# Reordered stages, later projection products and a row-by-row last product in a two-layer graph kernel on one Trainium2 core

## The chip, the cores and the metric

The kernel runs on one core of a Trainium2 chip. A core has five engines with instruction streams of their own: TensorE (PE, matrix products into PSUM), VectorE (DVE), ScalarE (ACT), GpSimd (POOL) and SyncE (SP, here only a queue that starts transfers). Each engine works through its own stream in order and waits on semaphores where it needs what another engine makes. The metric is the device time of one execution in microseconds (us); lower is better. The timed value is the median of several executions.

## The reference

Two graph layers act on `x` (4096 x 512) with one 4096 x 4096 adjacency matrix, everything in float32:

```python
def _L0_gnn_ref(cur, incidence_m):
    mask = incidence_m > 0
    head = mask.astype(incidence_m.dtype)
    head = head / jnp.maximum(jnp.sqrt(jnp.sum(head * head, axis=-1, keepdims=True)), EPS)
    inc = incidence_m + head
    return (inc @ cur) / jnp.sum(inc, axis=-1, keepdims=True)

def _L1_gnn_ref(X, A, W):
    A2 = A + jnp.eye(A.shape[0], dtype=A.dtype)
    dscale = jnp.diagonal(A2) ** (-0.5)
    temp = A2 @ X @ W.T
    A_norm = dscale[:, None] * A2 * dscale[None, :]
    return jax.nn.relu(A_norm @ temp)

x = _layernorm(x + _L0_gnn_ref(x, adj), axis=-1)
x = _layernorm(x + _L1_gnn_ref(x, adj, L1_gnn_W), axis=-1)
```

So there are three large products: `inc @ cur`, `A2 @ X`, and `A_norm @ temp`. The product by `W.T` (512 x 512) lies between the second and the third.

## The kernel before

**Tiling.** The first product (line 526 in the profile) uses one level of a Strassen-Winograd scheme: 7 products of blocks in place of 8. The second and third product (line 295) use two levels. The outer level has 7 products `p`, the inner level 7 products `m`. The work of these two phases is one list of steps `(k, s, p, kk)`: `k` is 2 for `A2 @ X` and 3 for `A_norm @ temp`, `s` is one of two strips, `p` runs through `ORDER[k]` (for `k = 3`: 2, 3, 5, 1, 6, 7, 4), and `kk` runs from 0 to 7 over the contraction. A step issues 7 matmuls, one for each inner product `m`, of 128 x 128 stationary values and 512 moving columns, into PSUM banks 0 to 6 (`q0` to `q6`). A float32 matmul stands in the profile as two records. After `kk = 7` the function `outer` combines the seven banks into the result blocks `c11, c12, c21, c22` on DVE.

**Bank 7.** The eighth PSUM bank (`spare`, line 96) serves everything else that PE does: the products by `W.T` (line 829) and the transposes of finished blocks (`turn_back`, line 903). There is one of it, so the next user waits until ACT has read the one before it.

**The order of a step** is written out by hand (`manual_schedule`); no scheduler moves anything. In the loop of line 1101 step `n` issues: loads; `prepare(n + 2)`, three DVE additions (lines 170, 172, 173) that make the sums for the matmuls two steps ahead; `sum_b` for the stationary side; operations put off by `outer` (`deferred`, line 1115, each over 128 x 2048 values); the 7 matmuls, between which `between[m]` puts other PE work ahead of matmul `m`; what is left of `items`; and then, lines 1144 to 1146, one further stage of the output rows under way.

**Rows under way.** When a block of the third product is finished, its rows leave through `layer1` (line 922): transposes on PE into bank 7, `rectify` on ACT (line 907, reads bank 7), then two stages, each run in a later step: `measured` (DVE: add the residual, line 758, and take statistics, lines 936 and 937) and `rest` (ACT: square root, line 940; DVE: reciprocal `rs` and offset `nb`, lines 162 and 164; ACT: `o*rs+nb`, line 165; a store). In the last product of all (`p = 4` of the last strip, `end` is true) up to two items are taken per step: one ahead of matmul 3, one after the matmuls. Its last rows go through `layer1_first` (line 945: transposes of the finished half, ACT line 957, and the stages `divided`, ACT line 962, and `rest`, DVE lines 758 and 970).

**Products by `W.T`.** `project` (line 813) is a generator. Two blocks are under way per outer product, one begun at `kk = 2` (`first`) and one at `kk = 4`. Each yields small tables `{m: product}` that say ahead of which matmul of the step a product goes. The seven products of a block are spread over three steps; ACT copies each from bank 7 (line 831); POOL makes four sums of blocks (line 836 and on) between the first table and the second; DVE combines the seven copies at the end (lines 858 to 867).

**The end.** For the last `TAIL = 4` steps of the last product no matmuls are issued in the loop; `finish` (line 973) does them product by product: `multiply(m)` runs the four remaining matmuls of one inner product, and DVE and ACT combine each while the next runs. The last one, `q4` (index 6), is needed for one quarter of the block. After it DVE subtracts it (line 1069), PE transposes four blocks of 128 x 128 (`turn`, line 993), and DVE and ACT take the layer norm (lines 1001 to 1023) and store through SP (line 1025).

Of the kernel before, what the change touches and what calls it, by code (L numbers as in the profile page):

```python
# [10 lines left out]
AF = mybir.ActivationFunctionType  # L11
ALU = mybir.AluOpType

P = 128
# [6 lines left out]
B11, B21, B22, T1, T2, T3, T4 = range(7)  # L21
# [5 lines left out]
def tile_adj_resnorm_d2(  # L27
# [37 lines left out]
    nc = tc.nc  # L65
# [12 lines left out]
    NQ = NB // 4  # L78
# [13 lines left out]
    def bank(m):  # L92

        return psum.tile([P, D], F32, tag=f"q{m}", name=f"q{m}")
# [4 lines left out]
    def row_tile(tag, bufs, shape=(P, D)):  # L99
        return rows.tile(list(shape), F32, tag=tag, name=tag, bufs=bufs)  # L100


    ident = const.tile([P, P], F32, name="ident")
# [76 lines left out]
    TAIL = 4  # L180
# [14 lines left out]
    steps = [(k, s, p, kk) for k in (2, 3) for s in range(NS) for p in ORDER[k] for kk in range(NQ)]  # L195
# [3 lines left out]
    resident, loaded, ready, raw_b, sums_b = {}, {}, {}, {}, {}  # L199
    made = {"a": 0, "s": 0, "load": 0, "load_b": 0}  # L200
    going, leaving = [], []
    queue, pairs, later, deferred, raises, stores = [], [], [], [], [], []
# [87 lines left out]
    def multiply2(n, acc, between):  # L290
        kk = steps[n][3]
        for m, (right, left) in enumerate(factors(n)):
            if m in between:
                between[m]()
            nc.tensor.matmul(acc[m], left, right, start=(kk == 0), stop=(kk == NQ - 1))  # L295

    def load_up_to(n):
        while made["load"] <= min(n, len(steps) - 1):
# [243 lines left out]
    def take(h, acc):  # L542

        y = row_tile("z", 2)
        nc.scalar.copy(y[:, 0:H], acc[0][:, 0:H])
        nc.scalar.copy(y[:, H:D], acc[1][:, 0:H])
        nc.scalar.copy(degrees[0][:, h:h + 1], acc[0][:, H:H + 1])
        return y
# [67 lines left out]
    ps = spare()  # L616
# [3 lines left out]
    for c in range(NC):  # L620
        m = count_half(0, c, ps)
# [135 lines left out]
    def add(o, y):  # L757
        nc.vector.tensor_add(o, o, y)  # L758
# [54 lines left out]
    def project(h, s, n, first):  # L813

        cols = slice(n * P, (n + 1) * P)
        a11, a12, a21, a22 = (C_of[2][h][f][:, 2 * r:2 * r + 2, cols] for r in range(2) for f in range(2))
        if first:
            pools["places"] = [t[:, i * H:(i + 1) * H] for t in (row_tile(t, 1) for t in ("p1", "p5", "u2", "u3")) for i in range(2)]  # L820

        places = [pools["places"][i] for i in (range(7) if first else (7, 1, 0, 6, 3, 2, 4))]
        q = []

        def product(left, right):
            def now():
                ps = spare()[:, 0:H]
                for e in range(2):
                    nc.tensor.matmul(ps, left[:, e, :], wt[:, right, e, :], start=(e == 0), stop=(e == 1))
                q.append(places[len(q)])  # L830
                nc.scalar.copy(q[-1], ps)
            return now

        def sums():
            s1, s2, s3, s4 = (y[:, 2 * i:2 * i + 2, :] for y in (row_tile("y", 2, (P, 4, P)) for _ in range(2)) for i in range(2))
            nc.gpsimd.tensor_add(s1, a21, a22)  # L836
            nc.gpsimd.tensor_add(s2, a11, s1)
            nc.gpsimd.tensor_add(s3, a11, a21)
            nc.gpsimd.tensor_add(s4, a12, s2)
            return s1, s2, s3, s4  # L840

        if first:
            yield {1: product(a11, B11), 3: product(a12, B21), 5: product(a22, T4)}
            s1, s2, s3, s4 = sums()
            yield
            yield {1: product(s2, T2), 3: product(s3, T3), 5: product(s1, T1)}
            yield
            yield {1: product(s4, B22)}
        else:
            yield {4: product(a11, B11)}  # L850
            s1, s2, s3, s4 = sums()
            yield
            yield {1: product(a12, B21), 3: product(a22, T4), 5: product(s2, T2)}
            yield
            yield {1: product(s3, T3), 3: product(s1, T1), 5: product(s4, B22)}
        q1, q2, q4, q6, q7, q5, q3 = q
        z = [row_tile("z", 2) for _ in range(2)]
        nc.vector.tensor_add(z[0][:, 0:H], q2, q1)
        nc.vector.tensor_add(q6, q6, q1)
        nc.vector.tensor_add(q7, q7, q6)  # L860
        nc.vector.tensor_add(q6, q6, q5)
        nc.vector.tensor_add(z[0][:, H:D], q3, q6)
        nc.vector.tensor_sub(z[1][:, 0:H], q4, q7)
        nc.vector.scalar_tensor_tensor(z[1][:, H:D], q7, -1.0, q5, op0=ALU.mult, op1=ALU.subtract)
        t = row_tile("t", 1, (P, 4, H))
        for r in range(2):
            nc.vector.tensor_sub(t[:, 2 * r, :], z[r][:, 0:H], z[r][:, H:D])
        leaving.extend(lambda r=r: leave_operands(h, r * NQ + s * SB + n, z[r], t[:, 2 * r, :]) for r in range(2))
        yield
# [103 lines left out]
    def finish(h, items, acc):  # L973

        c21 = C_of[3][h][0]
        q1, q2, q6, q5, q7, q3, q4 = range(7)
        p1, p5, u2 = (row_tile(t, 1) for t in ("p1", "p5", "u2"))
        e0, e1 = row_tile("y", 2), row_tile("y", 2)  # L980
        tail = [(steps[n][3], factors(n)) for n in range(len(steps) - TAIL, len(steps))]
        first = [items[r * SB][0] + h * NP for r in range(2)]
# [3 lines left out]
        def multiply(m, of=slice(0, TAIL)):  # L986
            for kk, f in tail[of]:
                right, left = f[m]
                nc.tensor.matmul(acc[m], left, right, start=False, stop=(kk == NQ - 1))  # L989

        def turn(r, n, i, o):

            nc.tensor.transpose(o, c21[:, 2 * r + i, n * P:(n + 1) * P], ident)  # L993
# [5 lines left out]
        def take(r, n, f, ps):  # L999
            y, o = rows_of(r, n)  # L1000
            nc.vector.scalar_tensor_tensor(o[:, :, f], ps, 0.0, y[:, :, f], op0=ALU.max, op1=ALU.add)

        def measure(r, n, i, w):
            nc.vector.bn_stats(late["st", r][:, n, i, :], rows_of(r, n // 2 * 2)[1][:, n % 2, i * w:(i + 1) * w])  # L1004

        def deviation(r, lo, hi):
            for n in range(lo, hi):
                nc.vector.bn_aggr(mean[r][:, n, :], late["st", r][:, n])
            nc.vector.tensor_add(dev[r][:, lo:hi], mean[r][:, lo:hi, 1], late["eps"][:, first[r] + lo:first[r] + hi])
            nc.scalar.activation(dev[r][:, lo:hi], dev[r][:, lo:hi], AF.Sqrt)  # L1010
# [6 lines left out]
        def leave(r, n, by_act):  # L1017
            o = rows_of(r, n // 2 * 2)[1][:, n % 2, :]
            rs = dev[r][:, n:n + 1]
            if by_act:  # L1020
                nc.scalar.activation(o, o, AF.Identity, scale=rs, bias=off[r][:, n:n + 1])  # L1021
            else:
                nc.vector.tensor_scalar(o, o, mean[r][:, n, 0:1], rs, op0=ALU.subtract, op1=ALU.mult)
            b = first[r] + n
            nc.sync.dma_start(out=out[b * P:(b + 1) * P, :], in_=o)
# [8 lines left out]
        nc.vector.tensor_sub(c21[:, 2, :], u2, c21[:, 2, :])  # L1034
        multiply(q5)
        nc.scalar.copy(p5, acc[q5])
        add(u2, p5)
        less(e1, u2, c21[:, 1, :])
        nc.vector.tensor_sub(c21[:, 3, :], u2, c21[:, 3, :])
        multiply(q3)  # L1040
        nc.vector.tensor_sub(c21[:, 1, :], e1, acc[q3])
        multiply(q7, slice(0, 1))

        for n in (0, 2):
# [3 lines left out]
                    turn(0, n + i, e, ps[:, i, e * P:(e + 1) * P])  # L1048
            take(0, n, slice(0, H), ps)
        multiply(q7, slice(1, TAIL))  # L1050
        for n in range(4):
            measure(0, n, 0, H)
        deviation(0, 0, 4)
# [1 line left out]
        invert(0, 0, 4)  # L1055
        for n in range(4):
            leave(0, n, True)
        nc.vector.tensor_add(c21[:, 2, :], c21[:, 2, :], acc[q7])

        multiply(q4, slice(0, TAIL - 1))  # L1060
        ps = bank(1).rearrange("p (n d) -> p n d", n=4)
        for n in range(4):
            turn(1, n, 1, ps[:, n, :])
        for n in (0, 2):
            take(1, n, slice(P, H), ps[:, n:n + 2, :])
        multiply(q4, slice(TAIL - 1, TAIL))
        for n in (0, 2):
            cols = slice(n * P, (n + 2) * P)
            nc.vector.tensor_sub(c21[:, 2, cols], c21[:, 2, cols], acc[q4][:, cols])  # L1069
        for n in (0, 2):  # L1070
            ps = bank((2, 3)[n // 2]).rearrange("p (n d) -> p n d", n=4)
            for i in range(2):
                turn(1, n + i, 0, ps[:, i, :])
                measure(1, n + i, 1, P)
            take(1, n, slice(0, P), ps[:, 0:2, :])
        for n in range(2):
            measure(1, n, 0, P)
        deviation(1, 0, 2)
        for n in range(2, 4):
            measure(1, n, 0, P)  # L1080
        invert(1, 0, 2)
        leave(1, 0, True)
        deviation(1, 2, 4)
        leave(1, 1, False)
        invert(1, 2, 4)
# [15 lines left out]
    for n, (k, s, p, kk) in enumerate(steps):  # L1101
# [10 lines left out]
        items = [queue.pop(0) for _ in range(min(len(queue), 2 if end else 1))] if 1 <= kk <= 6 else []  # L1112
        held = later[:]
        later.clear()
        while deferred:
            deferred.pop(0)()
            if not pairs:
                break
# [21 lines left out]
            load_b_up_to(n // 2 + 3)  # L1140
        for item in items:
            take_up(item)

        for stages in held if kk < NQ - 1 else ():
            stages.pop(0)()
        later[:0] = [stages for stages in held if stages]
        for pair in going[::-1]:
            next(pair)
        if kk in (4, 6):
# [72 lines left out]
```

## Time and profile before

| | |
|---|---|
| median of 3 runs | 2273.27 us (2271.16 to 2273.32) |
| the profiled execution | 2272.91 us, of which the span of its instructions is 2271.1 us |
| PE busy | 2251.0 us, 7382 matmul records |
| DVE / ACT / POOL busy | 1846.6 / 538.0 / 301.7 us |
| matmuls of the second and third product (line 295), mean of one record | 592 ns (128x512) |
| products by `W.T` (line 829), mean of one record | 380 ns (128x256) |
| transposes (lines 903, 993), mean of one record | 273, 281 ns (128x128) |
| DVE over 128x2048 (line 762, `less`) | 2.28 us |
| DVE `prepare` (lines 170, 172, 173), mean of each | 1236, 713, 701 ns |

[...] Matmuls overlap, so the distance from one start to the next is shorter: records of 512 columns start 0.43 us apart. "Idle before" is the time in which an engine waited in front of an instruction, with the instruction that released it.

### The profile page before, as it was taken

The numbers are of one execution on the slowest core, as the hardware profiler recorded it, in microseconds if no ns is written. First come the engines' busy times: TensorE is split into PE (matmuls) and PEld (weight loads), VectorE is DVE, ScalarE is ACT, GpSimd is POOL, SyncE is SP. The second block draws the span as 40 slices with busy tenths as digits, with TensorE's granted clock in tenths as the row PEclk, the third lists the DMA queues.
The fourth block names the chain that finished last, engine by engine and source line by source line (L and its number), as shares of the span: only waits on it lengthen the run. The fifth ranks groups of instructions, "written<-read, shape, count | busy, mean of one in ns | idle before, by whom it ended". The sixth has DMA issues, their size and how long they took to land. (4 is left out here: it accounts for less than half of the span.)

```text
span 2271.1 us, 22217 instructions
## 1 busy us (share of the span) xinstructions
PE 2251.0 (99%) x7382; PEld 1382.6 (61%) x7382; DVE 1846.6 (81%) x2620; ACT 538.0 (24%) x1336; POOL 301.7 (13%) x408
## 2 busy tenths in 40 slices
PE   8999999999999999999999999999999999999997
PEld 7888888888888844444555444555544444444443
DVE  6989999989989787888876887987767788766677
ACT  4346546555553000000111100111110011200013
POOL 0111122221121110002112200212210011100001
PEclk9999999999999999999999999999999999999999
DMA  9778888888876575675677767577776687765684
GB/s 311 259 273 289 264 265 285 283 279 285 268 248 218 199 278 207 220 294 186 250 274 217 236 255 258 186 285 269 216 239 226 235 288 278 254 242 221 224 295 153
DMA packets 177043, 568.27 MB, mean 250 GB/s; under 512 B 18064, under 2 KB 54944, under 8 KB 138528
## 3 DMA queue, kind: packets, MB, share of 16 engines
q1 hardware_dynamic: 128832, 459.32, 57.0%
q0 software_dynamic: 32480, 92.85, 13.2%
q10 hardware_dynamic: 15616, 14.69, 1.9%
q8 instruction: 58, 0.95, 0.2%
q14 instruction: 57, 0.47, 0.1%
HBM read 443.04 MB, written 123.74 MB: 250 GB/s over the span
## 5 line engine op out<-in xcount | busy, mean ns | idle before, releaser
L295 PE MATMUL q<-s,ts 128*128 128x512 f32 x1320 | 609.5, 592 | 0.2 <-DVE u L749 0.2
L526 PE MATMUL q<-b,s 128*128 128x256 f32 (+1 forms) x1920 | 453.4, 378 | 0.0
L295 PEld LDWEIGHTS q<-s,ts 128*128 128x128 f32 x1320 | 250.4, 190 | 297.8 <-issue 271.0
L170 DVE TENSOR_TENSOR s<-a 128x1024 f32<-128x1024 f32 x234 | 289.2, 1236 | 165.4 <-PE q L295 142.2
L526 PEld LDWEIGHTS q<-b,s 128*128 128x128 f32 x1920 | 362.7, 189 | 52.0
L526 PE MATMUL q<-b,a 128*128 128x256 f32 (+1 forms) x1440 | 350.5, 379 | 0.0
L295 PE MATMUL q<-a,tr 128*128 128x512 f32 x688 | 327.5, 592 | 0.0
L526 PEld LDWEIGHTS q<-b,a 128*128 128x128 f32 x1440 | 272.7, 189 | 38.3
L295 PE MATMUL q<-s,tr 128*128 128x512 f32 x440 | 224.7, 592 | 0.0
L295 PEld LDWEIGHTS q<-a,tr 128*128 128x128 f32 x688 | 128.8, 190 | 142.1 <-issue 134.9
L350 ACT ACTIVATE nat<-nat,tiny 128x512 f32<-128x512 f32 x240 | 173.4, 723 | 27.3 <-DMA nat<-adj 21.0
L295 PE MATMUL q<-a,ts 128*128 128x512 f32 x344 | 175.9, 593 | 0.0
L172 DVE TENSOR_TENSOR s<-a,s 128x512 f32<-128x512 f32 x234 | 166.8, 713 | 8.0
L173 DVE TENSOR_TENSOR s<-a,s 128x512 f32<-128x512 f32 x234 | 163.9, 701 | 8.0
L747 ACT COPY p<-q 128x512 f32<-128x512 f32 x27 | 15.8, 584 | 649.2 <-PE q L295 649.2
L501 DVE TENSOR_TENSOR a<-a,mask 128x1024 f32<-128x1024 f32 (+1 forms) x127 | 154.5, 1217 | 6.4
L499 DVE SCALAR_TENSOR_TENSOR mask<-a,sc 128x1024 f32<-128x1024 f32 (+2 forms) x129 | 154.2, 1197 | 2.2
L295 PEld LDWEIGHTS q<-s,tr 128*128 128x128 f32 x440 | 83.6, 190 | 91.6 <-issue 81.6
L411 ACT ACTIVATE nat<-nat 128x512 f32<-128x512 f32 x192 | 118.8, 619 | 14.0 <-DMA nat<-adj 13.9
L295 PEld LDWEIGHTS q<-a,ts 128*128 128x128 f32 x344 | 65.2, 190 | 83.0 <-issue 77.5
L836 POOL TENSOR_TENSOR y<-c,c 128x256 f32<-128x256 f32 x16 | 21.5, 1342 | 640.7 <-DVE c L762 391.3
L170 DVE TENSOR_TENSOR s<-r 128x1024 f32<-128x1024 f32 x48 | 59.8, 1245 | 40.5 <-PE q L295 31.8
(218 smaller groups left out, 2121.1 us busy)
## 6 DMA issues: line engine op xcount, KB each, us to landing
a<-adj_r SPq DMA_DIRECT2D x112, 1024.0 KB, 7.1
a<-oa SPq DMA_DIRECT2D x80, 1024.0 KB, 5.4
nat<-adj SPq DMA_DIRECT2D x240, 256.0 KB, 5.9
a<-adj_q SPq DMA_DIRECT2D x60, 1024.0 KB, 6.3
tr<-ob SPq DMA_DIRECT2D x112, 512.0 KB, 4.0
oa<-r SPq DMA_DIRECT2D x32, 1024.0 KB, 9.8
oa<-sr POOLq DMA_DIRECT2D x60, 512.0 KB, 6.8
y<-x POOLq DMA_DIRECT2D x64, 256.0 KB, 5.3
```

The costliest lines, as they stand in the source:

```text
L170: nc.vector.tensor_add(s[:, S3:S1 + 1, :], a[:, A11:A22 + 1, :], a[:, A21, :].unsqueeze(1).to_broadcast([P, 2, w]))
L172: nc.vector.tensor_add(s[:, S2, :], a[:, A11, :], s[:, S1, :])
L173: nc.vector.tensor_add(s[:, S4, :], a[:, A12, :], s[:, S2, :])
L295: nc.tensor.matmul(acc[m], left, right, start=(kk == 0), stop=(kk == NQ - 1))
L350: nc.scalar.activation(y, a, AF.Sign, bias=tiny, scale=2.0 ** 64, accum_out=accum)
L411: nc.scalar.activation(nat, nat, AF.Copy, accum_out=totals[j][:, h, t:t + 1])
L499: nc.vector.scalar_tensor_tensor(m, v, 0.0, s.unsqueeze(1).to_broadcast(list(v.shape)), op0=ALU.is_gt, op1=ALU.mult)
L501: nc.vector.tensor_add(z, z, y)
L526: nc.tensor.matmul(acc[m][:, 0:w], left, b[:, right, 0:w], start=(kk == 0), stop=(kk == NP - 1))
L747: nc.scalar.copy(p1, q1)
L836: nc.gpsimd.tensor_add(s1, a21, a22)
```

## The change

Four edits in the function's body:

1. In the last product (`end`) the stages of rows under way (`go_on`) are issued at the beginning of the step, after `prepare` and `sum_b` and ahead of `deferred`, of the matmuls and of new items. In every other product they stay after the items.
2. `project` issues its products later: the block begun at `kk = 2` has its seven products as 2, 3 and 2 per step in place of 3, 3 and 1; the block begun at `kk = 4` has its first one ahead of matmul 5 in place of 4.
3. The accumulation of `q4` in bank 6 ends four steps early; DVE subtracts that part ahead of `q7` (`c21[:, 2] - acc[q4]`). ACT negates the stationary side of the last four steps in place.
4. In `finish` the last four steps of `q4` are made by `complete_rows(n)` for four row blocks of 128: four matmuls of 128 moving columns with the operands exchanged, so that the result comes out transposed, then two matmuls by the identity that add `c21[:, 2]` and a copy `p7` of `q7`. They replace four matmuls of 512 columns, four transposes, and three DVE operations. The DVE operations behind them stand in a new order.

```diff
--- before.py
+++ after.py
@@ -292,7 +292,9 @@
         for m, (right, left) in enumerate(factors(n)):
             if m in between:
                 between[m]()
-            nc.tensor.matmul(acc[m], left, right, start=(kk == 0), stop=(kk == NQ - 1))
+
+            last = NQ - 1 - (TAIL if n >= len(steps) - NQ and m == 6 else 0)
+            nc.tensor.matmul(acc[m], left, right, start=(kk == 0), stop=(kk == last))
 
     def load_up_to(n):
         while made["load"] <= min(n, len(steps) - 1):
@@ -840,14 +842,14 @@
             return s1, s2, s3, s4
 
         if first:
-            yield {1: product(a11, B11), 3: product(a12, B21), 5: product(a22, T4)}
+            yield {3: product(a11, B11), 5: product(a12, B21)}
             s1, s2, s3, s4 = sums()
             yield
-            yield {1: product(s2, T2), 3: product(s3, T3), 5: product(s1, T1)}
+            yield {1: product(a22, T4), 3: product(s2, T2), 5: product(s3, T3)}
             yield
-            yield {1: product(s4, B22)}
+            yield {1: product(s1, T1), 3: product(s4, B22)}
         else:
-            yield {4: product(a11, B11)}
+            yield {5: product(a11, B11)}
             s1, s2, s3, s4 = sums()
             yield
             yield {1: product(a12, B21), 3: product(a22, T4), 5: product(s2, T2)}
@@ -974,9 +976,10 @@
 
 
 
+
         c21 = C_of[3][h][0]
         q1, q2, q6, q5, q7, q3, q4 = range(7)
-        p1, p5, u2 = (row_tile(t, 1) for t in ("p1", "p5", "u2"))
+        p1, p5, u2, p7 = (row_tile(t, 1) for t in ("p1", "p5", "u2", "u3"))
         e0, e1 = row_tile("y", 2), row_tile("y", 2)
         tail = [(steps[n][3], factors(n)) for n in range(len(steps) - TAIL, len(steps))]
         first = [items[r * SB][0] + h * NP for r in range(2)]
@@ -1034,11 +1037,15 @@
         nc.vector.tensor_sub(c21[:, 2, :], u2, c21[:, 2, :])
         multiply(q5)
         nc.scalar.copy(p5, acc[q5])
+
+        for left in (sums_b[n // 2][:, :, 3, :] for n in range(len(steps) - TAIL, len(steps), 2)):
+            nc.scalar.activation(left, left, AF.Copy, scale=-1.0)
         add(u2, p5)
         less(e1, u2, c21[:, 1, :])
         nc.vector.tensor_sub(c21[:, 3, :], u2, c21[:, 3, :])
         multiply(q3)
         nc.vector.tensor_sub(c21[:, 1, :], e1, acc[q3])
+        nc.vector.tensor_sub(c21[:, 2, :], c21[:, 2, :], acc[q4])
         multiply(q7, slice(0, 1))
 
         for n in (0, 2):
@@ -1048,6 +1055,7 @@
                     turn(0, n + i, e, ps[:, i, e * P:(e + 1) * P])
             take(0, n, slice(0, H), ps)
         multiply(q7, slice(1, TAIL))
+        nc.scalar.copy(p7, acc[q7])
         for n in range(4):
             measure(0, n, 0, H)
         deviation(0, 0, 4)
@@ -1055,31 +1063,39 @@
         invert(0, 0, 4)
         for n in range(4):
             leave(0, n, True)
-        nc.vector.tensor_add(c21[:, 2, :], c21[:, 2, :], acc[q7])
-
-        multiply(q4, slice(0, TAIL - 1))
+
+        def complete_rows(n, ps):
+
+            cols = slice(n * P, (n + 1) * P)
+            for i, (kk, f) in enumerate(tail):
+                right, left = f[q4]
+                nc.tensor.matmul(ps, right[:, cols], left, start=(i == 0), stop=False)
+            nc.tensor.matmul(ps, c21[:, 2, cols], ident, start=False, stop=False)
+            nc.tensor.matmul(ps, p7[:, cols], ident, start=False, stop=True)
+
+
+        ends = [bank(b).rearrange("p (n d) -> p n d", n=4) for b in (2, 3)]
+        complete_rows(0, ends[0][:, 0, :])
         ps = bank(1).rearrange("p (n d) -> p n d", n=4)
         for n in range(4):
             turn(1, n, 1, ps[:, n, :])
         for n in (0, 2):
             take(1, n, slice(P, H), ps[:, n:n + 2, :])
-        multiply(q4, slice(TAIL - 1, TAIL))
-        for n in (0, 2):
-            cols = slice(n * P, (n + 2) * P)
-            nc.vector.tensor_sub(c21[:, 2, cols], c21[:, 2, cols], acc[q4][:, cols])
-        for n in (0, 2):
-            ps = bank((2, 3)[n // 2]).rearrange("p (n d) -> p n d", n=4)
+        complete_rows(1, ends[0][:, 1, :])
+        take(1, 0, slice(0, P), ends[0][:, 0:2, :])
+        for n in range(2):
             for i in range(2):
-                turn(1, n + i, 0, ps[:, i, :])
-                measure(1, n + i, 1, P)
-            take(1, n, slice(0, P), ps[:, 0:2, :])
-        for n in range(2):
-            measure(1, n, 0, P)
+                measure(1, n, i, P)
+        for n in (2, 3):
+            complete_rows(n, ends[1][:, n - 2, :])
         deviation(1, 0, 2)
-        for n in range(2, 4):
-            measure(1, n, 0, P)
+        for n in (2, 3):
+            measure(1, n, 1, P)
+        take(1, 2, slice(0, P), ends[1][:, 0:2, :])
         invert(1, 0, 2)
         leave(1, 0, True)
+        for n in (2, 3):
+            measure(1, n, 0, P)
         deviation(1, 2, 4)
         leave(1, 1, False)
         invert(1, 2, 4)
@@ -1112,6 +1128,14 @@
         items = [queue.pop(0) for _ in range(min(len(queue), 2 if end else 1))] if 1 <= kk <= 6 else []
         held = later[:]
         later.clear()
+
+        def go_on():
+
+            for stages in held if kk < NQ - 1 else ():
+                stages.pop(0)()
+            later[:0] = [stages for stages in held if stages]
+        if end:
+            go_on()
         while deferred:
             deferred.pop(0)()
             if not pairs:
@@ -1140,10 +1164,8 @@
             load_b_up_to(n // 2 + 3)
         for item in items:
             take_up(item)
-
-        for stages in held if kk < NQ - 1 else ():
-            stages.pop(0)()
-        later[:0] = [stages for stages in held if stages]
+        if not end:
+            go_on()
         for pair in going[::-1]:
             next(pair)
         if kk in (4, 6):
```

## Prediction

> **What bounds the kernel now.** I read the first page, then the waits of PE, then the timeline in three places where the change acts.
>
> ```profile
> PE 2251.0 (99%) x7382; PEld 1382.6 (61%) x7382; DVE 1846.6 (81%) x2620; ACT 538.0 (24%) x1336; POOL 301.7 (13%) x408
> ...
> PE q L370 <- ACT sr L350: 6.2, 1, 6.2
> PE q L829 <- DVE c L787: 1.1, 2, 0.8
> PE q L903 <- ACT o L907: 1.0, 1, 1.0
> ...
> PE q L993 <- DVE c L1069: 0.5, 1, 0.5
> PE q L989 <- DVE c L172: 0.5, 1, 0.5
> ```
>
> PE is busy for 99% of the span. Its idle time is the start (6.2 us), the layer norm after its last matmul, and the small waits above. So the change can gain only these waits and some of the end, and every microsecond by which it holds PE up is lost. The columns of the waits are total, times and longest. The wait of 1.0 us stands in the second step (`kk = 1`) of the last product:
>
> ```profile
> 2215.38 2.28 DVE L762 SCALAR_TENSOR_TENSOR c<-c,c 128x2048 f32<-128x2048 f32 x1
> 2217.59 0.16 DVE L162 RECIPROCAL rs<-sd 128x1 f32<-128x1 f32 x1
> 2217.78 0.16 DVE L164 SCALAR_TENSOR_TENSOR nb<-mv,rs 128x1 f32<-128x1 f32 x1
> 2217.97 0.82 ACT L165 ACTIVATE o<-o,nb,rs 128x512 f32<-128x512 f32 x1 [14.02 <-DVE nb L164]
> 2218.70 0.67 ACT L907 ACTIVATE o<-q,dscale 128x512 f32<-128x512 f32 x1
> ...
> 2219.41 1.21 DVE L170 TENSOR_TENSOR s<-a 128x1024 f32<-128x1024 f32 x1
> 2219.41 0.66 PE L903 MATMUL q<-ident,c 128*128 128x128 f32 x4 [0.96 <-ACT o L907]
> ...
> 2221.99 0.16 DVE L162 RECIPROCAL rs<-sd 128x1 f32<-128x1 f32 x1
> 2222.18 0.16 DVE L164 SCALAR_TENSOR_TENSOR nb<-mv,rs 128x1 f32<-128x1 f32 x1
> ...
> 2222.37 0.82 ACT L165 ACTIVATE o<-o,nb,rs 128x512 f32<-128x512 f32 x1 [1.35 <-DVE nb L164]
> ```
>
> Four rows are under way here: A and B from the product before, C and D taken in this step. ACT stands at A's line 165 until DVE has made A's `nb`, which comes after the long `less` (L762). C's `rectify` (L907 at 2218.70) is next in ACT's stream, and D's transposes need bank 7, so PE waits. B's `nb` is made at 2222.18, after the `prepare` of 2219.41, and B's line 165 follows at 2222.37.
>
> ```profile
> 2264.00:2265.00 1.00, 0.00 (x0) 0.00 (x0) 0.97 (x5) 0.86 (x2) 0.00 (x0) 0.98 0.00 0
> 2265.00:2266.00 1.00, 0.00 (x0) 0.00 (x0) 0.84 (x4) 0.57 (x2) 0.00 (x0) 0.50 0.19 74
> ```
>
> These are windows; the third number from the end is PE's clock. PE's last matmul begins before 2262; the clock falls to half at 2265, some 3.2 us later.
>
> [...] The trace shows records of 190 ns, but two such loads behind a transpose take 0.30 us together (PEld at 2233.57), so the second begins 0.11 us after the first[...].
>
> **Edit 2, products by W.T.** The two waits of 1.1 us (0.32 and 0.77) stand ahead of the product at matmul 1 of `kk = 2`, which needs DVE's L787. At matmul 3 it comes two matmuls (1.7 us) later; both waits go: -1.1 us. Number and kind of products stay. Behind a later product wait ACT's copy and then DVE's combination: the seventh copy of the first block comes 1.7 us later. At the first place DVE reaches the combination at 1076.40, while the copy ended at 1071.4, so it would still be in time. POOL's sums are used two matmuls later as well. DVE prepares a step or more ahead and waits for PE here (174.0 us in all at L170), which covers the rest. If that cover is gone, DVE is held by up to 1.7 us, not PE. Cost taken: 0 (0 to +1).
>
> **Edit 1, rows under way.** New order on DVE in `kk = 0`: `prepare`; A's `rs`, `nb`; B's `measured`; `less`. In `kk = 1`: `prepare`, then B's `rs`, `nb`. New order on ACT: A's square root and line 165; B's square root and line 165; only then C's and D's `rectify`. Before, C and D stood ahead of B. The total of DVE up to B's `nb` is unchanged (the same instructions in another order), so B's `nb` stays at 2222.18 and B's line 165 at 2222.37. C's `rectify` follows 0.73 later (2217.97 to 2218.70 before), at 2223.10, and D's transposes 0.71 after that (2218.70 to 2219.41), at 2223.81 in place of 2219.41. So the wait isn't removed but grows by **4.4 us**, to 5.4 us of idle PE. Everything on PE moves with it.
>
> In `kk = 3` the like happens on a small scale. ACT now has C's and D's line 165 and four activations of `divided` (0.61 each) ahead of the first L957. I follow it: `prepare` waits for the sums that PE used in `kk = 2` (free at about 2230.1); it ends at 2232.8; C's line 165 begins at 2233.2; D's square root, `nb` and line 165 at 2234.6; `divided` from 2235.3 to 2237.75; L957 0.6. The next transposes, due at 2233.24 + 4.4 = 2237.64, begin at 2238.4: **+0.75 us** (0 to 1.5). In return DVE is now ahead of PE in `finish`. Before, PE needed 2256.30 - 2233.68 = 22.62 us from its first matmul there to the end of `q7`; its work in it is 48 records at 0.429 and 8 transposes at 0.107, 21.45. The waits of 1.18 us (L172, L1041) go: **-1.2 us**.
>
> **Edits 3 and 4, the end.** Removed after `q7`: 8 records of 512 columns (3.43 us), and, behind the last of them, DVE L1069 (0.75) and four transposes. Added: 4 row blocks of 8 + 4 records of 128 columns. No such float32 record is in the trace. Below: the stream of 128 columns is a quarter of 0.429, 0.107[...], so 12 records take 1.285 us. Above: load and stream without overlap at the load's record, 0.190, so 2.28 us. I take 0.107, because the transposes, which also load 128 columns each, run at 0.107 (four in 0.44). Four blocks and four transposes: 4 x 1.285 + 0.43 = 5.57 us after `q7`, where the matmuls ended at 2260.17, 3.87 after. But less follows. After the last row block: 0.21 to the `take`, then by the durations of before (take 0.33, reciprocal and offset 0.26, two statistics 0.39, two aggregates 0.39, sum 0.16, L1023 0.54, reciprocal and offset 0.40) 2.4 us to the last ACT activation, 0.82 long. That is 5.57 + 0.21 + 2.4 + 0.82 = 9.0 us after `q7`; before it was 2266.30 - 2256.30 = 10.0. **-1.0 us**, and up to +3.0 with the slower records (48 x 0.083 = 4.0). The copy of `q7` on ACT (0.6 us) is covered by eight records (0.86 us); negations and subtraction lie beside `q3` and `q7`. The way from there to the end (4.8 us, stores) I leave.
>
> **Sum** for the profiled execution: -1.1 + 4.4 + 0.75 - 1.2 - 1.0 = +1.85 us, that is 2274.8 from 2272.91. The median is 0.36 above that execution: 2273.27 + 1.85 = 2275.1.
>
> **The clock.** [...] No gap of that length in mid-run is in the trace before. [...]2275.1 + 1.7 = **2276.8 us**.
>
> **Rivals.**
> - The gap without the clock: 2275.1 us. [...] Against: three executions or more are timed, and their median lies between.
> - The other side, slower: records of 128 columns run at the load's 0.190 us. Place: the four row blocks; price +4.0 us, thus 2279.1 without the clock's fall and 2280.8 with it. It decides from 0.056 us more per record (2.7 us over 48) upward, a distance of 0.163 us. For it: records of 190 ns. Against: two such loads start 0.11 us apart.
> - The gap doesn't come, since B's line 165 doesn't stand ahead of C: then 1.1 (W.T), 1.0 (L903), 1.0 (end) and up to 1.2 (`finish`) are gained, some 2269.5 us. For it: DVE makes A's `nb` 2.2 us earlier. Against: B's `nb` still stands behind `less` and `prepare`.
>
> **How the numbers follow.** Gap with the clock's fall 0.47; gap without it 0.33; slow records 0.12; no gap 0.08. A median of this kernel tells about 0.2%, 4.5 us, from no change: below 2268.7 is faster, above 2277.8 slower. Slower: the slow records, and a quarter of the first case[...]: 0.24. Faster: 0.03. Same: 0.73. The range from 2273.0 to 2279.6 leaves out the case without a gap and most of the slow records with a cold clock.
>
> **What would show it.** In the profile after: PE's wait on ACT's rectify at D's transposes of about 5.4 us (near 0 if I am wrong), with B's line 165 directly ahead of C's rectify on ACT; the waits on L787 gone; a clock of 0.5 behind the gap, or not; row blocks of 1.3 us (2.3 in the slow case); waits on L172 and L1041 in `finish` gone. The prediction is wrong if B's `nb` comes before 2219, or if the row blocks take over 2 us.

## The result, and the profile after

The changed kernel takes 2276.85 us (median of 15 runs, 2275.39 to 2278.75), the kernel before 2272.50 us (median of 15 runs, 2271.16 to 2273.94). The ratio is 1.0019, 95% interval 1.0012 to 1.0026: 4.35 us slower, at the edge of what was called no change. The profiled execution of the changed kernel took 2277.67 us, its span is 2275.9 us, 4.8 more than before. Lines of the source below the change stand 2 or more higher (`rectify` is now L909, `less` L764, L1041 is L1047).

First the busy times on the page after:

```profile
PE 2253.7 (99%) x7418; PEld 1387.0 (61%) x7418; DVE 1847.4 (81%) x2618; ACT 538.0 (24%) x1339; POOL 293.9 (13%) x408
```

PE is busy 2.7 us longer than before. It has 36 records more, those of the row blocks at the end, and part of the time is the clock, below. PE's waits after (columns: total, times, longest):

```profile
PE q L372 <- ACT sr L352: 6.3, 2, 6.2
PE q L905 <- ACT o L909: 5.3, 1, 5.3
PE q L831 <- ACT p L833: 1.9, 2, 1.1
PE q L905 <- ACT o L959: 0.5, 1, 0.5
```

The waits on DVE L787, L172 and L1041 are gone. In their place stand one wait of 5.3 us and one of 0.5, which were forecast, and two of 1.9 together, which were not. The timeline of the second step of the last product, ACT and PE after:

```profile
2216.53 0.81 ACT L165 ACTIVATE o<-o,nb,rs 128x512 f32<-128x512 f32 x1 [11.81 <-DVE nb L164]
2218.08 0.29 ACT L942 ACTIVATE sd<-mv,eps_t 128x1 f32<-128x1 f32 x1 [0.74 <-DVE mv L939]
2223.11 0.81 ACT L165 ACTIVATE o<-o,nb,rs 128x512 f32<-128x512 f32 x1 [4.73 <-DVE nb L164]
2223.83 0.67 ACT L909 ACTIVATE o<-q,dscale 128x512 f32<-128x512 f32 x1
...
2224.55 1.11 PE L905 MATMUL q<-ident,c 128*128 128x128 f32 x4 [5.34 <-ACT o L909]
2225.46 3.04 PE L297 MATMUL q<-a,tr 128*128 128x512 f32 x4
...
2229.19 0.60 PE L905 MATMUL q<-ident,c 128*128 128x128 f32 x4
```

Before, D's transposes stood at 2219.41, and PE went on with

```profile
2219.91 1.88 PE L295 MATMUL q<-a,tr 128*128 128x512 f32 x4
...
2222.48 0.60 PE L903 MATMUL q<-ident,c 128*128 128x128 f32 x4
```

Row A's scaling (2216.53) is early now. But row B's (2223.11) stands ahead of C's `rectify`, and it waits 4.73 us for B's offset. D's transposes wait for that. The four records at 2225.46 take 3.04 us in place of 1.88, and the next transposes come 4.64 us after D's in place of 3.07. That is the clock, by windows (third number from the end):

```profile
2223.00:2224.00 1.00, 0.00 (x0) 0.00 (x0) 0.90 (x3) 0.89 (x2) 0.00 (x0) 1.00 0.98 410
2224.00:2225.00 1.00, 0.45 (x2) 0.45 (x3) 0.96 (x2) 0.50 (x1) 0.78 (x2) 0.68 0.98 401
2225.00:2226.00 1.00, 1.00 (x5) 0.80 (x4) 0.97 (x2) 0.25 (x1) 1.00 (x3) 0.50 0.93 356
...
2227.00:2228.00 1.00, 1.00 (x3) 0.43 (x2) 0.97 (x3) 0.00 (x0) 1.00 (x3) 0.61 0.90 315
```

A share of 0.68 means that the clock was at half for 0.64 of that microsecond. Read from the shares of 0.68 and 0.61 in this way, it is at half from 2224.36 to 2227.78, 3.42 us, beginning 0.2 us before PE goes on. And one row block of the end, in the chain that ended last (start, length):

```profile
2263.43 0.70 DVE c L760
2264.12 0.04 issue
2264.17 0.66 PE q L996 x4
2264.83 0.89 PE q L1072 x8
2265.72 0.22 PE q L1073 x2
2265.94 0.22 PE q L1074 x2
```

A row block is 0.89 + 0.22 + 0.22 = 1.33 us, or 0.111 us for a record of 128 columns.

### The profile page after: what moved, and what is told of

The parts are those of the page before. It is cut to its first block, busy times and chain, and to the rows that moved or that the text cites. A ratio compares the mean times of both kernels' runs of the same rounds, so it can differ in the third digit from the quotient of the medians.

```text
span 2275.9 us, 22289 instructions
## 1 busy us (share of the span) xinstructions
PE 2253.7 (99%) x7418; PEld 1387.0 (61%) x7418; DVE 1847.4 (81%) x2618; ACT 538.0 (24%) x1339; POOL 293.9 (13%) x408
## 5 line engine op out<-in xcount | busy, mean ns | idle before, releaser
L172 DVE TENSOR_TENSOR s<-a,s 128x512 f32<-128x512 f32 x234 | 165.5, 707 | 8.0
L297 PE MATMUL q<-r,tr 128*128 128x512 f32 x192 | 92.2, 592 | 0.0
```

The source lines that it names most:

```text
L172: nc.vector.tensor_add(s[:, S2, :], a[:, A11, :], s[:, S1, :])
```

## The experiments

All times are medians; the ratio to the kernel before has its 95% interval.

| kernel | us | ratio |
|---|---|---|
| changed kernel | 2276.85 | 1.0019 [1.0012, 1.0026] |
| e1 changed, edit 1 undone | 2270.15 | 0.9991 [0.9982, 0.9999] |
| e2 edit 1 alone | 2278.95 | 1.0026 [1.0016, 1.0036] |
| e3 edit 2 alone | 2271.87 | 0.9998 [0.9989, 1.0006] |
| e4 edits 3 and 4 alone | 2270.94 | 0.9992 [0.9984, 1.0000] |
| e5 stages early in the first step only | 2269.45 | 0.9988 [0.9981, 0.9994] |
| e6 early stages ahead of `prepare` | 2273.00 | 0.9999 [0.9990, 1.0007] |
| e7 gap filled with zero products | 2274.70 | 1.0011 [1.0004, 1.0017] |
| e8 e5, stores of a block later | 2282.88 | 1.0045 [1.0032, 1.0058] |
| e9 e5, edit 2 undone | 2269.98 | 0.9987 [0.9981, 0.9993] |
| e10 e5, stores of a block together | 2279.32 | 1.0025 [1.0015, 1.0035] |

### Which edit costs the time: e1 to e4

e1 undoes edit 1 in the changed kernel:

```diff
-        if end:
-            go_on()
...
-        if not end:
-            go_on()
+        go_on()
```

> The changed kernel with edit 1 alone undone: stages of rows under way again behind the new items in the last product. If the early stages are the cost (my theory), PE's wait on ACT's rectify at the transposes of row D falls from 5.3 us to about 1.0, the clock stays at 1.0, the wait of 0.5 us in the fourth step goes, and some 1.1 us of waits on L172 and L1047 come back: about 5.4 us less than the changed kernel, 0 to 2 us below the kernel before. The rival, that the row blocks or the later products cost the time, leaves it 3 us or more above the kernel before.

> The kernel before with edit 1 alone. My theory: a wait of PE of 5.3 us at the transposes of row D, the clock at half for about 3 us behind it, 0.5 us in the fourth step, 1.1 us of waits in the finish gone: 5.0 to 6.0 us slower than before. The rival (the other edits cost the time): at most 2 us slower.

The waits of PE with edit 1 undone (e1):

```profile
PE q L905 <- ACT o L909: 1.0, 1, 1.0
...
PE q L992 <- DVE c L172: 0.4, 1, 0.4
PE q L831 <- ACT p L833: 0.2, 1, 0.2
```

The wait of 1.0 us is back in place of 5.3, and the kernel takes 6.7 us less than the changed one, more than the 5.4 that I expected. Part of the excess isn't edit 1: the waits on ACT's copy (L833) are 0.2 us in this profile and 1.9 in that of the changed kernel, with the same edit 2 in both. Edit 1 alone (e2) is 6.45 us slower than before, also more than the 5 to 6 expected. Its profile has the same wait of 5.3 us at D's transposes and the same 0.5 in the fourth step, and the clock is at half for 6.8 us, 3.8 of them while PE works. From D's transposes to the next ones e2 takes 4.90 us, 1.83 more than before, where I had allowed about 1.5 for the clock. So edit 1 is the loss.

e3 is edit 2 alone, the tables of `project` as in the change:

> The kernel before with edit 2 alone. The prediction's step: the two waits on DVE L787 (1.1 us) go, nothing comes: 1.1 us faster. My theory since the result: DVE is the late one there, and the wait reappears on ACT's copy at the product ahead of matmul 5 of the fourth step of the block (kk = 5), which stands behind the scalings that wait for DVE; the waits on L787 go and 0.5 to 2 us of waits on ACT come at the same two places; net between 0.9 us faster and 0.3 us slower.

It measures 0.63 us faster, with an interval that holds no change. The waits on L787 are gone; one wait of 0.5 us on ACT's copy (L831) has come, at the first of the two places only.

e4 is the changed kernel with edits 1 and 2 undone:

> The kernel before with edits 3 and 4 alone. Prediction: row blocks of 1.3 us each, no more than 0.12 us per record of 128 columns, and the end 1.0 us sooner. The rival of slow records: blocks of 2.3 us and 3 us slower. From the profile after (0.6 us less between the end of q7 and the last activation, 0.9 us less from there to the end) I expect 0.6 to 1.6 us faster.

1.56 us faster, at the upper end of what was expected; the interval just touches 1. The rival of slow records is out: in every profile with row blocks, eight records take 0.89 us. The medians of e2, e3 and e4 add up to 6.45 - 0.63 - 1.56 = +4.26 us, where the whole change is +4.35. Each of the three is uncertain by about 2 us, so this shows no interaction of the edits but can't exclude a small one.

### The place in the queue: e5

```diff
-        if end:
-            go_on()
+        early = end and kk == 0
+        if early:
+            go_on()
...
-        if not end:
+        if not early:
             go_on()
```

> The changed kernel, but the stages go to the beginning of the step only in the first step of the last product (kk = 0), where no new item is taken; in the later steps they stay behind the new items. My theory: A's offset is made ahead of the long DVE operation, so that C's rectify isn't held (the wait of 1.0 us at row D's transposes goes), and B's scaling stands behind C and D (no wait of 5.3 us, clock stays at 1.0): 1 us less than with all stages late, 6 us less than the changed kernel, 1.5 to 3 us below the kernel before. The rival, that ahead of the long DVE operation the stages delay the half-block that the third step transposes, shows as a wait of PE on DVE L764 of 1 us or more and no gain over all stages late.

The timeline of ACT and PE in e5:

```profile
2215.84 0.81 ACT L165 ACTIVATE o<-o,nb,rs 128x512 f32<-128x512 f32 x1 [11.81 <-DVE nb L164]
2216.57 0.67 ACT L909 ACTIVATE o<-q,dscale 128x512 f32<-128x512 f32 x1
2219.06 0.69 ACT L909 ACTIVATE o<-q,dscale 128x512 f32<-128x512 f32 x1 [1.82 <-issue]
2219.64 0.28 ACT L942 ACTIVATE sd<-mv,eps_t 128x1 f32<-128x1 f32 x1
...
2218.37 0.60 PE L905 MATMUL q<-ident,c 128*128 128x128 f32 x4
```

A's scaling comes ahead of the long `less`, C's `rectify` follows at once, and B's square root stands behind C and D. D's transposes have no idle time before them. 2269.45 us is 7.4 us less than the changed kernel and 0.7 less than e1 (1 expected; the intervals of the two overlap). The rival didn't show: no wait on L764. Edit 1 was right in the step where no new row is taken, and wrong in the next.

### The clock behind a shorter and a filled gap: e6 and e7

e6 calls `go_on` ahead of `prepare` in the last product, so that B's offset comes sooner and PE's gap is shorter. The question is whether the clock then stays at 1.0:

```diff
-        if n + LA < len(steps):
-            prepare(n + LA)
-        if n % 2 == 0 and n // 2 + 1 < len(groups):
-            sum_b(n // 2 + 1)
...
         if end:
             go_on()
+        if n + LA < len(steps):
+            prepare(n + LA)
+        if n % 2 == 0 and n // 2 + 1 < len(groups):
+            sum_b(n // 2 + 1)
```

> The changed kernel with the early stages moved ahead of prepare as well. DVE then makes B's offset 2.6 us sooner, so the wait of PE at row D's transposes is 2.7 us in place of 5.3. [...]it stays at 1.0 here: 2.6 + 1.5 = about 4.1 us less than the changed kernel, and some 0.5 more if the wait in the fourth step shrinks. If the clock falls after shorter gaps too, it is only 2.6 us less and the windows behind the gap show 0.5.

PE's gap in e6, in the timeline:

```profile
2220.32 0.66 PE L905 MATMUL q<-ident,c 128*128 128x128 f32 x4 [2.76 <-ACT o L909]
2220.81 3.35 PE L297 MATMUL q<-a,tr 128*128 128x512 f32 x4
```

The windows behind it:

```profile
2221.00:2222.00 1.00, 1.00 (x2) 0.34 (x2) 1.00 (x2) 0.69 (x1) 1.00 (x3) 0.54 1.12 401
...
2224.00:2225.00 1.00, 1.00 (x3) 0.43 (x2) 0.86 (x4) 0.00 (x0) 0.23 (x1) 0.75 1.00 397
```

The gap is 2.76 us as expected, but the clock fell all the same, at about 2221.1, when PE had gone on for 0.8 us, and came back at 2224.5. The time is 3.85 us less than the changed kernel, near the 4.1 that I expected for a clock that stays, so the total alone would have misled: in this profile PE has no waits at all among the products by `W.T`, where the changed kernel's had 1.9 us, and none in the fourth step, where it had 0.5.

e7 fills the gap of the changed kernel with work of no effect:

```diff
+        if end and kk == 1:
+            filler = ready[n][0][:, A11, :]
...
+        if end and kk == 1:
+            for _ in range(6):
+                nc.tensor.matmul(acc[0], zeros, filler, start=False, stop=False)
         for item in items:
             take_up(item)
...
+            zeros = late["pool"].tile([P, P], F32, name="zeros")
+            nc.gpsimd.memset(zeros, 0.0)
```

> The changed kernel with six matmuls of 512 columns by a stationary block of zeros, accumulated into bank 0 (adding nothing), ahead of row D's transposes: 5.1 us of PE work in the gap of 5.3 us. If the halved clock behind the gap costs 1.6 us, it goes: the clock stays at 1.0 and the time is 1.3 to 1.6 us below the changed kernel. If the gap alone costs the time, nothing changes (within 0.3 us).

In e7's windows from 2216 to 2233 the clock is 1.00 throughout, and the four records behind D's transposes take 1.88 us again:

```profile
2217.74 5.31 PE L1169 MATMUL q<-a,zeros 128*128 128x512 f32 x12
2223.24 0.66 PE L905 MATMUL q<-ident,c 128*128 128x128 f32 x4 [0.19 <-ACT o L909]
2223.74 1.88 PE L297 MATMUL q<-a,tr 128*128 128x512 f32 x4
```

The median is 2.15 us below the changed kernel's, more than the 1.3 to 1.6 expected. The two intervals overlap, so the windows show the cause better than the medians show its size. It isn't one lucky execution: the mean clock over the span is 0.998 in all 15 runs of the changed kernel, and 0.999 or 1.000 in all 21 of e7.

### The wait that moved: e8, e9, e10

Behind a block's products ACT scales and stores it (`leave_operands`) ahead of matmuls 2 and 4 of `kk = 5`; the copy that the product ahead of matmul 5 needs stands between. In the profile after, ACT and PE at the first place:

```profile
1080.78 0.72 ACT L880 ACTIVATE z<-z,dscale 128x512 f32<-128x512 f32 x1 [2.21 <-DVE t L869]
...
1083.03 0.37 ACT L833 COPY p<-q 128x256 f32<-128x256 f32 x1 [1.13 <-issue]
...
1083.55 1.10 PE L831 MATMUL q<-wt,y 128*128 128x256 f32 x4 [1.10 <-ACT p L833]
```

The same copy and product before:

```profile
1082.04 0.37 ACT L831 COPY p<-q 128x256 f32<-128x256 f32 x1 [1.14 <-PE q L829]
1082.86 1.03 PE L829 MATMUL q<-wt,y 128*128 128x256 f32 x4
```

ACT waits for DVE's `t`, then scales, issues three stores, and only then copies. Before, that copy ended at 1082.41 and PE came at 1082.86: 0.45 us of slack. The changed kernel takes 0.32 us of it by removing PE's first wait, and in this execution DVE came to the block 1.13 us later against PE (its L789 begins at 1051.46, L787 before at 1050.33, while PE's preceding records start within 0.01 us of each other): 0.45 - 0.32 - 1.13 = -1.0, and PE waited 1.1.

How late DVE comes differs from one execution to the next, and the ten profiles with the stores at their old places show what edit 2 does about it. "Late" is the start of L789 (L787) less that of the PE record `a,ts` near 1050; the wait is PE's at this first place, in us:

| without edit 2 | late | wait | with edit 2 | late | wait |
|---|---|---|---|---|---|
| e2 | -0.77 | 0 | e1, e5 | -0.77, -0.76 | 0 |
| before | -0.14 | 0.32 | e6 | -0.07 | 0 |
| e9 | 0.00 | 0.46 | e7 | +0.17 | 0.29 |
| e4 | +0.99 | 1.45 | e3 | +0.43 | 0.55 |
| | | | changed kernel | +0.98 | 1.10 |

Where there is a wait, it is the lateness plus 0.46 us without edit 2, and plus 0.12 with it. Edit 2 makes the wait at this place 0.34 us shorter, and doesn't remove it.

e8 moves the stores in e5 to matmuls 4 and 6:

```diff
-            between[2], between[4] = leaving
+            between[4], between[6] = leaving
```

> The kernel of early stages in the first step only, with the scalings and stores of a finished block (leave_operands) two matmuls later in the step kk = 5 (ahead of matmuls 4 and 6 in place of 2 and 4), so that the product ahead of matmul 5 no longer has its copy's predecessor behind them. My theory of the moved wait: the waits of PE on ACT's copy (1.9 us in two places in the profile after) go, 0.5 to 2 us less than without this edit. The rival: the next wait is at the first product of the step after (kk = 6), with the same size, and nothing is gained.

The waits on ACT's copy are gone as expected, which shows that the scalings and stores held the copy. But e8 is 13.4 us slower than e5, which neither theory had. DVE's waits in this phase and PE's waits, in e8:

```profile
DVE z L865 <- DMA ob<-z: 18.0, 5, 5.8
...
PE q L297 <- DVE y L750: 4.1, 2, 2.6
PE q L297 <- DVE c L750: 3.6, 2, 2.4
```

`z` has two buffers, one for each half of a block. The next block's half waits on the store that now leaves later, DVE reaches the seven banks of the outer product late, and PE waits for them. Two of these gaps, 2.58 and 2.39 us, halve the clock as well, from 1164.4 and from 1290.7 for 3.4 us each.

e9 undoes edit 2 in e5; e10 puts both stores ahead of matmul 4.

> The kernel of early stages in the first step only (2269.45 us), with edit 2 undone: the products by W.T at their old places. If edit 2 trades the waits on DVE L787 (0.6 to 1.9 us in the profiles) for shorter ones on ACT's copy (0.2 to 1.9 us), this is 0.3 to 1.2 us slower, with waits on L789 back and none on ACT L833. If edit 2 gains nothing, the two are equal within 0.3 us.

> The kernel of early stages in the first step only, with both scalings and stores of a finished block ahead of matmul 4 of the step kk = 5 (in place of 2 and 4). The stores end no later than before by more than a microsecond, so DVE's wait for the two buffers of the block (18.0 us where they were two matmuls later) stays small; the copy ahead of matmul 5 no longer stands behind the scalings, so PE's wait on ACT L833 (0.6 us in that profile) goes: 0 to 0.6 us faster. The rival: the buffers are tight by less than a microsecond, DVE waits for the stores again, and it is 2 us or more slower.

e9 measures 0.9987 [0.9981, 0.9993] where e5 has 0.9988 [0.9981, 0.9994]: no difference, though the intervals, over 2 us wide, can't exclude the 0.3 to 1.2 us of the first theory. Its profile has 0.9 us of waits on L789 and none on ACT, e5's has 0.6 on ACT and none on L789. Edit 2 exchanges one wait for another that is somewhat shorter. e10 is 9.9 us slower than e5: the rival held, DVE again waits for the stores (14.9 us in four places). Delaying even the first half's store, by two matmuls, is too much. Nor did PE's waits on ACT's copy go, as I had expected: three of 1.0 us together stand in its profile, the first (0.29) ahead of matmul 1 of `kk = 6`: the product there waits for the copy that now stands behind the scalings and stores. So the wait moved by one product.

## Why the prediction was right

The direction, the place and the mechanism came out as written, and 2276.8 against 2276.85 us is closer than the steps deserve: errors of both signs cancelled, and that is luck. In the profiled executions:

| step | predicted | profile |
|---|---|---|
| products by W.T, up to D's transposes | -1.1 | +0.8 |
| wait at D's transposes | +4.4 | +4.38 (5.34 - 0.96) |
| clock behind it | +1.7 | +1.57 (D's transposes to the next: 4.64, before 3.07) |
| wait in the fourth step | +0.75 | +0.49 |
| waits in `finish` | -1.2 | -1.10 (21.52, before 22.62) |
| `q7` to the last activation | -1.0 | -0.57 (9.43, before 10.00) |
| from there to the end of the span | 0 | -0.94 (3.86, before 4.80) |

**Edit 1** was right in each part, with sizes within 0.3 us. The long gap was found by following one queue that is worked off in order, ACT's: B's scaling in front of C's `rectify`, and B's offset behind `less` and `prepare` on DVE. e1, e2 and e5 show that this place, and no other edit, is the loss.

**Edit 2** is the step that failed. The prediction counted both waits as gained and let DVE's slack cover the rest; it looked at PE and DVE ahead of the block's end, and not at ACT, which holds the copy in `kk = 5` behind scalings that wait for the same late DVE. The slack there was 0.45 us, so that at the first place the edit makes the wait 0.34 us shorter and doesn't remove it. e3 and e9 measure the edit at nothing that can be told (0.63 us faster, and none), and the +0.8 of the one profile is mostly how late DVE came in that execution: e6 and e7, with the same products, have 0 and 0.3 us of such waits in place of 1.9. The prediction also said that without such cover DVE would be held and not PE; it was PE.

**Edits 3 and 4.** A record of 128 columns takes 0.111, not 0.107 us (0.2 us over 48). DVE's addition of `q7` to `c21[:, 3]` stood 0.51 us until ACT had copied `q7`, so that the transposes between the first two row blocks began 0.2 us late. Together these are the missing 0.4. The stores of the end took 0.94 us less, which the prediction had left at nothing: from the last activation to the end of the span are 3.8 to 3.9 us in the profiles of the changed kernel, e1, e4, e5, e6, e7 and e9, and 4.6 to 4.8 in those without edits 3 and 4 (before, e2, e3). Why is not shown. e4's 1.56 us is about the sum of both, 0.57 + 0.94.

**The clock.** It fell, and 1.57 us came where 1.7 was taken. The 1.7 was my estimate: the trace before has no gap of that length in mid-run, and shows the clock at half only at its end, from 2265 on. How likely the fall was, that trace doesn't show either: no number of it stands behind the 0.47 and 0.33 given to the gap with the fall and without. In both profiles in which PE stood idle for 5.34 us (the changed kernel, e2) the clock fell, and so it did behind gaps of 2.76 us (e6), of 2.58 and 2.39 (e8) and of 2.32 (e10); the rival "gap without the clock" shows in no profile with a gap of 5.3 us. The size isn't the same each time: behind the same gap of 5.34 us the clock was at half for 3.42 us in the changed kernel and for 6.8 in e2 (3.8 of them while PE works), and the way from D's transposes to the next was 1.57 and 1.83 us longer than before.

**The base.** The median of before over more runs is 2272.50, 0.77 us below the three that the forecast stood on. The change is +4.35, where +3.5 was forecast.

## What to carry to other kernels

Before moving work to the front of a step, list what it puts ahead of what on *every* engine it issues to, and for each moved instruction ask when the last of its inputs is made: here B's scaling, 0.81 us long, stood 4.73 us for its input on ACT, and C's `rectify` came behind it. A wait removed from the engine that bounds the kernel is gained only as far as the next slack on the same late producer, here 0.34 us. And where the clock fell behind D's gap on TensorE, the way to the next transposes took 1.57 to 1.83 us longer than before, beside the gap itself (1.57 in the changed kernel and 1.83 in e2, with gaps of 5.34 us; 1.70 in e6, with 2.76).

## What the runs showed of the hardware

In the middle of the run TensorE's clock fell to half at gaps of 5.34 us (the changed kernel, e2), 2.76 (e6), 2.58 and 2.39 (e8) and 2.32 (e10), and not at one of 0.96 (before, at D's transposes). It was at half for 3.42 us in the changed kernel, for 3.4 in e6 and at both gaps of e8, and for 6.8 in e2. But the length of the gap doesn't decide alone. In e10 a gap of 2.40 us left the clock at 1.00, and one of 2.32 us in the same execution halved it:

```profile
1223.83 1.13 PE L297 MATMUL q<-r,tr 128*128 128x512 f32 x2 [2.40 <-DVE c L750]
1286.57 1.50 PE L297 MATMUL q<-a,tr 128*128 128x512 f32 x2 [2.32 <-DVE c L750]
```

Two records take 1.13 us behind the longer gap and 1.50 behind the shorter one. The clock around both is the third number from the end:

```profile
1222.33:1225.75 3.42, 1.92 (x5) 0.96 (x6) 3.18 (x6) 1.06 (x3) 3.42 (x5) 1.00 1.02 381
1225.75:1229.16 3.41, 3.41 (x10) 1.50 (x9) 3.31 (x5) 0.00 (x0) 3.33 (x4) 1.00 1.03 318
1283.77:1287.18 3.41, 1.09 (x4) 0.31 (x3) 3.27 (x5) 2.22 (x6) 3.00 (x4) 1.00 0.99 315
1287.18:1290.59 3.41, 3.41 (x6) 1.45 (x5) 3.17 (x5) 0.00 (x0) 1.30 (x2) 0.50 0.93 253
```

In e7 twelve records of matmuls by a block of zeros, 5.31 us in the place of the gap, went with a clock of 1.00 from 2216 to 2233. Float32 records of 128 columns, load and stream together, go 0.111 us apart in the changed kernel (12 in 1.33 us), though the load's record is 0.19 us long.
